# First stage of a four-layer graph network: where x is loaded, how the layernorms are ordered, and when the check of adj is written

## The chip, the core and the metric

The kernel runs on one core of one Trainium2 chip. The metric is the device time of a launch in microseconds, as the median of seven runs. The engines are named as the profile names them: PE (matrix products), DVE (vector), ACT (scalar activations), POOL (GpSimd) and SP (which here only issues DMAs).

## What is computed

Four layers work on x, 8 batches of 2048 nodes with 64 features, with a 0/1 matrix `adj` of 2048 x 2048. Each layer first normalises x. Cut to what this change touches:

```python
def _layernorm(x, axis=-1, eps=1e-5):
    m = jnp.mean(x, axis=axis, keepdims=True)
    v = jnp.var(x, axis=axis, keepdims=True)
    return (x - m) / jnp.sqrt(v + eps)

# layer 0
h = jnp.maximum(_layernorm(x, axis=-1), 0.0)
x = x + _L0_gnn_ref(h, L0_gnn_H, adj, 64, L0_gnn_W, ...)   # begins with h @ W
# layers 1, 2 and 3 follow in the same manner, each with adj
```

## The kernel before

The program has a first stage and a long rest. The first stage, `start` (L629), does three things: it normalises x for layer 0, multiplies the result by `W` (`features`, L669), and reads `adj` once to see whether it is sparse enough for a faster form of the layers (`check_adj`, L368). The check ends in one integer, `flag` (L423). Every engine loads the flag and branches on it (L3187, L3214), so that nothing of the rest begins before the flag is written and before that engine has done its own part of the first stage. The rest is not touched by the change.

**The layernorms.** x lies as 4 pairs of batches on 128 partitions and is cut into 4 chunks of 512 nodes. For each chunk `ch`, `load_x` (L262) loads 1 MB into the tile `x_ch` (two buffers), and `norm_parts` (L284) runs: for each of 4 pairs PE subtracts the mean by a product with `center`, ACT squares the result into `sq` (L291), and DVE or ACT in turn take its positive part `xr` (L294, L296); PE sums the squares (`to_rows`), ACT takes the root `std` (L299), DVE its reciprocal (L300). There the generator yields. Its second part spreads the reciprocal over the partitions by PE (`from_rows`) and multiplies on DVE (`write`, L641). Before, `norm` runs both parts without a stop, and `xr`, `sq` and `std` have one buffer each.

**The features.** For a chunk, PE multiplies by `ww` in two layouts, and ACT copies both out (L676 into `h_t`, L682 into `h_n`).

**The check of adj.** A loop over 16 row tiles of 1 MB. SP loads tile t into one of four halves of two buffers `rows` (L390). ACT squares it into `squares`, of which there are four (L391). DVE compares the square with the row (L392), which proves that the entries are 0 or 1. POOL clears the diagonal (L395) and issues the DMA that stores the tile as `links` in device memory (L399). PE counts blocks (`seen`). So the load of tile t + 4 waits for the compare of tile t, and the squares of tile t + 4 wait for the store of tile t. After the loop come small sums, two counting products, and `flag`.

**The order.** Each engine runs its instructions in a fixed order. A scheduler makes that order when the program is built: it takes the instructions in the order in which they are written as their rank, and lets a later one go first where it estimates that the engine would stand idle. In the kernel before, the loop over chunks was written first (with `features` of chunk ch - 1 after the layernorm of chunk ch), then the check, then `features` of the last chunk. SP's order before was: two loads of x, a load `own` of the diagonal (8 KB in pieces of 4 bytes), 2 rows of adj, x of chunk 2, 4 rows, x of chunk 3, 6 rows, `hm` (0.5 MB of H), 4 rows.

Of the kernel before, what the change touches and what calls it, by code (L numbers as in the profile page):

```python
# [7 lines left out]
F = mybir.dt.float32  # L8
# [11 lines left out]
P = 128  # L20
# [3 lines left out]
NP = NB // 2  # L24
NT = N // P
R = P // NP
CW = 512
NC = N // CW
TC = CW // P
# [106 lines left out]
class Kernel:  # L136
# [39 lines left out]
    def mm(self, out, lhsT, rhs, start=True, stop=True):  # L176
        self.nc.tensor.matmul(out, lhsT, rhs, start=start, stop=stop)  # L177
# [102 lines left out]
    def norm(self, *args):  # L280
        for _ in self.norm_parts(*args):
            pass
# [346 lines left out]
    def start(self, pool, slots):  # L629

        nc, tc, a = self.nc, self.tc, self.a
        self.deg = pool.tile([P, 2, NT], F, name="deg")
        self.edges = pool.tile([P, NT, FAR], BF, name="edges")
        self.self_weight = pool.tile([P, NT], F, name="self_weight")
        flag = pool.tile([1, 1], I32, name="flag")
        with tc.tile_pool(reuse_waits="tile", name="k00", bufs=1) as k:
            ww = self.block_diag(k, a["W"], "ww")
            hn = Halves(slots, "hn", ("q0", "q1"), False)

            def write(q, ch, xr, scale):  # L640
                nc.vector.tensor_mul(hn(q)[:, ch * CW : (ch + 1) * CW], xr, scale)  # L641

            with (
                tc.tile_pool(reuse_waits="tile", name="links_ps", bufs=1, space=PSUM) as lps,
                tc.tile_pool(reuse_waits="tile", name="ln", bufs=2) as w,
                tc.tile_pool(reuse_waits="tile", name="ln_ps", bufs=6, space=PSUM) as ps,
            ):
                seen = lps.tile([P, NT, FAR], F, name="seen")
                self.h = (
                    hn, Halves(slots, "h_t", ("q2", "q3"), False),  # L650
                    Halves(slots, "h_n", ("q4", "q5"), True),
                )

                def bank():
                    return ps.tile([P, CW], F, name="bank")

                for ch in range(NC):
                    x = self.load_x(w, 0, ch)
                    xr = w.tile([P, NP, CW], F, name="xr", bufs=1)
                    sq = w.tile([P, NP, CW], F, name="sq", bufs=1)  # L660
                    std = w.tile([P, CW], F, name="std", bufs=1)
                    self.norm(ch, x, xr, sq, std, bank, write)
                    if ch > 0:
                        self.features(ww, ch - 1, bank)
                self.check_adj(k, slots, seen, lps, flag)
                self.features(ww, NC - 1, bank)
        return flag

    def features(self, ww, ch, bank):  # L669
# [2612 lines left out]
```

## Time and profile before

| | |
|---|---|
| median of 7 runs | 1923.02 us |
| lowest and highest of the 7 | 1910.75 and 1927.65 us |
| the profiled execution: its time | 1915.7 us |
| its span, first to last instruction | 1913.9 us |
| PE, DVE, ACT, POOL busy over the span | 1685.5, 1380.1, 817.9, 1082.6 us |
| `flag` written in the trace | at 96.5 us |
| first stage's last PE product and last ACT copy | at 99.6 and 100.2 us |

Times inside the trace are microseconds from the start of the span. A row of the timeline view gives the start, the duration, the engine, the line, the operation, what it writes and reads, how many were merged (`x4`), and in brackets how long the engine stood idle before it and what ended that. The window view gives the busy time of each engine in a stretch, then the granted PE clock as a share of full speed, the share of the 16 DMA engines that was busy, and GB/s.

### The profile page before, as it was taken

What the parts mean: (1) busy time and instruction counts of PE and PEld (TensorE: products, weight loads), DVE (VectorE), ACT (ScalarE), POOL (GpSimd) and SP (SyncE); (2) the same over time, 40 slices, a digit from 0 to 9 for tenths busy, and PEclk for the clock granted to TensorE, in tenths of its full rate; (3) what the DMA queues carried; (4) which work ended last, traced back from release to release, by engine and by line L of the source; (5) the groups of instructions that cost most, each with busy time, mean ns of one, the idle gap of its engine ahead of it and who ended that gap; (6) DMA issues with size and microseconds to landing.
All of it is one profiled execution on the core that took longest, in us unless ns stands there. A gap on an engine that the chain in (4) does not pass through costs nothing.

```text
span 1913.9 us, 22584 instructions
## 1 busy us (share of the span) xinstructions
PE 1685.5 (88%) x7139; PEld 962.4 (50%) x7139; DVE 1380.1 (72%) x2281; ACT 817.9 (43%) x1650; POOL 1082.6 (57%) x1039
## 2 busy tenths in 40 slices
PE   6888899998997788899999999879999899599794
PEld 2446766664334454344343434258677576355442
DVE  6887778884667877778888877556566676478683
ACT  5732544554666654222111010067676754286200
POOL 1101366776862645887687766547373641587743
PEclk8998999998998889899999999999999999799896
DMA  8741223334545775234132242168788774766745
GB/s 335 293 124 46 67 94 99 112 123 163 178 125 153 213 223 159 86 86 132 39 110 88 72 116 77 51 215 272 240 253 263 227 246 146 247 183 184 209 142 190
DMA packets 127371, 305.25 MB, mean 159 GB/s; under 512 B 29680, under 2 KB 33536, under 8 KB 122112
## 3 DMA queue, kind: packets, MB, share of 16 engines
q0 software_dynamic: 45328, 149.60, 27.0%
q1 hardware_dynamic: 79600, 149.82, 23.4%
q10 hardware_dynamic: 2304, 4.20, 0.6%
q8 instruction: 60, 0.98, 0.2%
q14 instruction: 79, 0.65, 0.1%
HBM read 240.41 MB, written 63.14 MB: 159 GB/s over the span
## 4 chain that ended last, share of the span: by engine, by line
PE 33%; DMA 6%; issue 6%; POOL 6%; DVE 4%; ACT 1%; SPq 0%; POOLq 0%; DVEq 0%; ACTq 0%
PE pk L177 17%; PE acc L177 10%; POOL ring L2975 3%; DMA raw<-sent,index 2%; DMA ring<-f_rows,near 2%; PE bank L177 1%; POOL raw L2645 1%; PE pn L177 1%; POOL half L1872 1%; PE pw L177 1%; PE pz L1955 1%; PE side L177 1%; DMA ring<-f_rows,order 1%; PE p L177 1%; POOL q L3154 1%
## 5 line engine op out<-in xcount | busy, mean ns | idle before, releaser
L2645 POOL DMA_INDIRECT raw<-sent,index x300 | 315.9, 1053 | 286.6 <-DVE part_lo L2663 142.7
L2662 ACT CAST part_hi<-raw 128x512 fp32r<-128x512 f32 x352 | 210.8, 619 | 300.4 <-PE acc L177 203.0
L2663 DVE TENSOR_TENSOR part_lo<-raw,part_hi 128x512 fp32r<-128x512 f32 x352 | 264.9, 772 | 93.3 <-ACT part_hi L2662 86.3
L177 PE MATMUL pk<-q,w 128*128 128x512 f32 (+1 forms) x768 | 305.6, 615 | 4.2 <-DVE q L1753 2.7
L1872 POOL TENSOR_TENSOR half<-half,y 128x512 f32<-128x512 f32 x210 | 263.5, 1285 | 63.5 <-DVE y L1867 62.8
L177 PE MATMUL acc<-q,ident 128*128 128x512 f32 x416 | 204.2, 619 | 19.8 <-DVE q L3058 14.7
L177 PEld LDWEIGHTS pk<-q,w 128*128 128x128 f32 (+1 forms) x768 | 115.9, 191 | 155.0 <-issue 109.5
L177 PE MATMUL acc<-part_hi,weights 128*128 128x512 f32 x365 | 172.8, 474 | 21.8 <-ACT part_hi L2662 21.0
L177 PE MATMUL acc<-part_lo,weights 128*128 128x512 f32 x365 | 164.1, 451 | 24.6 <-DVE part_lo L2663 24.2
L2975 POOL DMA_INDIRECT ring<-f_rows,near x121 | 147.9, 1222 | 60.9 <-issue 28.6
L1867 DVE SCALAR_TENSOR_TENSOR y<-pk,bias,q 128x512 f32<-128x512 f32 x210 | 148.1, 743 | 43.8 <-POOL half L1872 23.5
L177 PEld LDWEIGHTS acc<-q,ident 128*128 128x128 f32 x416 | 78.6, 197 | 95.4 <-issue 63.5
L2354 POOL TENSOR_TENSOR q<-q,beta 128x512 f32<-128x512 f32 x57 | 76.0, 1335 | 71.4 <-DVE beta L2330 32.6
L177 PEld LDWEIGHTS acc<-part_lo,weights 128*128 128x128 f32 x365 | 71.5, 196 | 81.3 <-DVE part_lo L2663 68.0
L177 PEld LDWEIGHTS acc<-part_hi,weights 128*128 128x128 f32 x365 | 71.2, 195 | 74.3 <-ACT part_hi L2662 39.9
L177 PE MATMUL pp<-adj,x_ind_hi 128*128 128x512 f32 x256 | 90.2, 468 | 0.5 <-DVE q L882 0.3
L3040 DVE TENSOR_TENSOR q<-ring,e 128x1024 f32<-128x1024 f32 x58 | 70.1, 1221 | 10.6 <-PE acc L177 10.5
L2631 ACT CAST hub_weights<-dense 128x384 fp32r<-128x384 uint8 x80 | 40.4, 511 | 84.3 <-PE acc L177 84.0
L300 DVE RECIPROCAL std<-std 128x512 f32<-128x512 f32 (+1 forms) x17 | 53.8, 3162 | 30.4 <-ACT std L299 30.4
L2354 POOL TENSOR_TENSOR q<-q,coef 128x512 f32<-128x512 f32 x57 | 63.0, 1106 | 21.0 <-DVE q L2377 17.6
L2562 POOL DMA_INDIRECT listed_raw<-in_adjT_dram,cell x60 | 63.8, 1063 | 16.5 <-issue 15.9
L177 PE MATMUL pp<-adj,x_ind_lo 128*128 128x512 f32 x256 | 72.7, 403 | 0.0
(503 smaller groups left out, 3425.1 us busy)
## 6 DMA issues: line engine op xcount, KB each, us to landing
rows<-in_adj_dram SPq DMA_DIRECT2D x16, 1024.0 KB, 9.0
adj_t<-in_adjT_dram SPq DMA_DIRECT2D x64, 256.0 KB, 3.0
own<-sent SPq DMA_DIRECT2D x52, 256.0 KB, 4.2
raw<-sent SPq DMA_DIRECT2D x52, 256.0 KB, 3.6
sent<-u SPq DMA_DIRECT2D x48, 256.0 KB, 3.3
q<-x SPq DMA_DIRECT2D x9, 1024.0 KB, 4.9
links<-squares POOLq DMA_DIRECT2D x16, 512.0 KB, 8.6
sent<-q SPq DMA_DIRECT2D x32, 256.0 KB, 3.5
```

The costliest lines, as they stand in the source:

```text
L177: self.nc.tensor.matmul(out, lhsT, rhs, start=start, stop=stop)
L300: nc.vector.reciprocal(std, std)
L1867: nc.vector.scalar_tensor_tensor(y, pks[b, half], bias[:, b : b + 1], emb[:, b], op0=OP.add, op1=OP.mult,)
L1872: nc.gpsimd.tensor_add(acc, acc, y)
L2354: self.nc.gpsimd.tensor_tensor(x, x, by.unsqueeze(2).to_broadcast([P, NB, D]), op=OP.mult)
L2562: self.kern.behind(nc.gpsimd.indirect_dma_start(raw[:, i], None, rows, bass.IndirectOffsetOnAxis(ap=self.cell[:, c + i : c + i + 1], axis= ...
L2631: self.nc.scalar.copy(to, self.lists.dense[:, :, i * P : (i + 1) * P])
L2645: self.nc.gpsimd.indirect_dma_start(raw, None, self.rows[:], bass.IndirectOffsetOnAxis(ap=self.lists.index[:, c : c + 1], axis=0),)
L2662: nc.scalar.copy(hi, raw)
L2663: nc.vector.tensor_sub(lo, raw, hi.bitcast(F))
L2975: self.nc.gpsimd.indirect_dma_start(to, None, self.kern.f_rows[:], bass.IndirectOffsetOnAxis(ap=index, axis=0))
L3040: nc.vector.tensor_tensor(y.rearrange("n i (b f) -> n i b f", b=NB), block[:, i : i + 2, : NB * D].rearrange("n i (b f) -> n i b f", b=NB) ...
```

## The change

All four loads of x are written ahead of everything else, and go into the memory that `h_n` will fill later, so that the tile `x_ch` is gone. The first part of the layernorm of chunk ch + 1 is written before the second part of chunk ch; `xr` and `std` have two buffers for this. `features` of chunk 0 and 1 are written inside the loop, and those of chunks 2 and 3 after the check.

```diff
+                h_n = self.h[2].tiles
+                xs = [h_n[c // 2][:, TC * (c % 2) : TC * (c % 2 + 1)] for c in (1, 0, 2, 3)]
                 for ch in range(NC):
-                    x = self.load_x(w, 0, ch)
-                    xr = w.tile([P, NP, CW], F, name="xr", bufs=1)
+                    nc.sync.dma_start(xs[ch], self.xs[0][ch])
+
+                def norm(ch):
+                    xr = w.tile([P, NP, CW], F, name="xr")
                     sq = w.tile([P, NP, CW], F, name="sq", bufs=1)
-                    std = w.tile([P, CW], F, name="std", bufs=1)
-                    self.norm(ch, x, xr, sq, std, bank, write)
-                    if ch > 0:
+                    std = w.tile([P, CW], F, name="std")
+                    return self.norm_parts(ch, xs[ch], xr, sq, std, bank, write)
+
+                norms = [norm(0)]
+                next(norms[0])
+                for ch in range(NC):
+                    if ch + 1 < NC:
+                        norms.append(norm(ch + 1))
+                        next(norms[-1])
+                    for _ in norms[ch]:
+                        pass
+                    if 0 < ch < NC - 1:
                         self.features(ww, ch - 1, bank)
                 self.check_adj(k, slots, seen, lps, flag)
-                self.features(ww, NC - 1, bank)
+                for ch in range(NC - 2, NC):
+                    self.features(ww, ch, bank)
```

What the scheduler makes of it: on every engine the instructions behind the branch stand in the same order as before; all differences lie in the first stage. SP's order is now: four loads of x, `own`, 4 rows, `hm`, 12 rows. DVE's order (multiplies means the four of L641 of a chunk, r4 the compare L392 of row tile 4): xr 0, reciprocal 0, xr 1, reciprocal 1, multiplies 0, r0, xr 2, multiplies 1, reciprocal 2, r1, `hm` to 0/1, r2, half of xr 3, r3, other half of xr 3, reciprocal 3, multiplies 2, r4, sum of `hm`, r5, multiplies 3, r6, r7, r8 to r15 with three small ones between, then the small sums. Before it was: xr 0, r0, reciprocal 0, r1, multiplies 0, r2, half of xr 1, r3, other half, reciprocal 1, r4, multiplies 1, r5 to r7, xr 2, reciprocal 2, r8, multiplies 2, r9 to r11, xr 3, reciprocal 3, r12, multiplies 3, r13 to r15, the small sums. PE's products for `features` now all end before the small counting products; before, those of chunk 3 stood behind them.

## The prediction, made before the changed kernel ran

> **What bounds the kernel now.** On every engine the instructions behind the branch on `flag` stand in the same order before and after, so the question is when the first stage ends. I read the window view over that stage first.
>
> ```profile
> 20.00:40.00 20.00, 12.63 (x72) 4.83 (x72) 19.05 (x17) 14.21 (x19) 3.55 (x8) 0.67 0.97 369
> 40.00:60.00 20.00, 16.94 (x120) 9.17 (x116) 14.58 (x16) 14.97 (x22) 3.32 (x8) 0.92 1.01 419
> 60.00:80.00 20.00, 16.88 (x121) 9.03 (x121) 17.78 (x19) 16.30 (x25) 3.71 (x8) 0.91 0.96 327
> 80.00:100.00 20.00, 19.36 (x139) 12.71 (x140) 17.10 (x41) 12.73 (x20) 4.84 (x11) 0.91 0.30 122
> ```
>
> The DMA engines are full (0.96 to 1.01) up to 80 us and nearly empty after it, and DVE is busy for 14.6 to 19.1 of every 20 us. So there are two bounds with little between them: first the transfers, then DVE with what is left over. PE's clock is the next column: 0.67 from 20 to 40.
>
> Next the waits of the DMA queue and of ACT up to 100 us (total, times, longest).
>
> ```profile
> SPq L390 <- DVE equal L392: 46.5, 11, 8.9
> SPq L264 <- PE bank L177: 7.4, 2, 4.7
> ACT squares L391 <- DMA rows<-in_adj_dram: 8.6, 3, 5.8
> ```
>
> Eleven loads of adj wait for a compare on DVE: how early DVE gets to the compares decides how early the transfers run. Then the timeline, at the first norm and at the end.
>
> ```profile
> 4.91 6.53 SPq L390 DMA_DIRECT2D rows<-in_adj_dram  x2
> 15.96 1.91 ACT L391 ACTIVATE squares<-rows 128x2048 bf16<-128x2048 f32 x1 [1.99 <-DMA rows<-in_adj_dram]
> 17.86 0.58 ACT L291 ACTIVATE sq<-bank 128x512 f32<-128x512 f32 x1
> 17.99 2.29 DVE L392 SCALAR_TENSOR_TENSOR equal<-rows,squares 128x2048 bf16<-128x2048 f32 x1 [3.30 <-ACT squares L391]
> 20.96 3.35 DVE L300 RECIPROCAL std<-std 128x512 f32<-128x512 f32 x1 [0.67 <-ACT std L299]
> 26.48 2.48 DVE L641 TENSOR_TENSOR q<-xr,bank 128x512 f32<-128x512 f32 x4
> 61.99 11.18 SPq L390 DMA_DIRECT2D rows<-in_adj_dram  x4
> ...
> 89.56 2.42 DVE L392 SCALAR_TENSOR_TENSOR equal<-rows,squares 128x2048 bf16<-128x2048 f32 x1
> 96.50 0.14 DVE L423 TENSOR_SCALAR flag<-one 1x1 int32<-1x1 f32 x1
> 96.76 2.84 PE L177 MATMUL bank<-ww,q 128*128 128x128 f32 x24
> 99.64 0.59 ACT L682 COPY q<-bank 128x512 f32<-128x512 f32 x1 [0.31 <-PE bank L177]
> 100.17 0.37 DVE L518 COPY raw<-bank 128x208 f32<-128x208 f32 x1 [0.89 <-PE bank L177]
> ```
>
> ACT's fourth square of norm 0 (17.86) stood behind the square of adj's row 0, which waited for its transfer. The last row was issued near 73 and landed at 81.6, but DVE compared it only at 89.56, since norm 3 and three compares stood before it: the end is DVE's. And PE and ACT still finish features up to 100.2, past the flag at 96.64.
>
> **What the change removes, adds and moves.** I walk DVE's new order with these durations: compare 2.29 + 0.08 = 2.37; reciprocal 3.35; four multiplies 2.48; two positive parts 2 x 0.69 = 1.38.
>
> *Norm 0 and 1.* No row of adj stands in ACT's way now. The fourth product by `center` is out at 14.2, as before. Square and positive part (0.6 each) end at 15.4, the table load of 1.28 at 16.7, the root (0.69) at 17.4, the reciprocal at 20.9; it was 24.3. ACT's six operations for norm 1 (3.5) end at 20.9, its root at 22.3; DVE does xr 1 meanwhile and reciprocal 1 to 25.8 (it was 38.2). Multiplies 0 end at 28.2. So norms run 3 and 12 us earlier.
>
> *Rows 0 to 3.* Two more transfers of x are now ahead of row 0: 1 MB at the 400 GB/s of these windows is 2.6 to 2.75 us each, so row 0 lands at 21.4, not 15.9. That costs nothing by itself, for DVE comes to compare 0 only at 28.2 and ends it at 30.6, not at 20.3. That is the price: row 4 is issued 10 us later.
>
> *Rows 4 to 10.* From 30.6: xr 2 1.38, multiplies 1 2.48, reciprocal 2 3.35, compare 1 to 40.2; the test of `hm` 0.69, compares 2 and 3 with xr 3 to 47.0; reciprocal 3 to 50.3, multiplies 2 to 52.8, compare 4 to 55.2, the sum of `hm` 1.21, compare 5 to 58.8, multiplies 3 and compare 6 to 63.6. All of this is DVE back to back. In such a chain DVE also waits for ACT and PE: in the two windows from 20 to 60 it idled 0.95 and 5.42. From both sides 0 to 6.4; I take 1.5, near the fuller window, as DVE has more ready work now. Compare 6 ends at 65.1, and row 10 is issued then; in the trace row 10 was issued at 48.7. In between the DMA engines drain: rows 5, 6, 7 are issued at 40.2, 43.2 and 46.3, one MB each, and each MB is gone in 2.5 us.
>
> *Rows 10 to 15.* From here DVE has nothing but compares (2.37 each) and the transfers are late: a tile is 1.05 MB of row and 0.52 MB of links, at 419 GB/s 3.75 us. Row 10 takes 5.7 from issue to landing (as row 12 before, 61.99 to 67.7) and lands at 70.8; five more tiles at 3.75 put row 15 at 89.6. Square 2.0 and compare 2.5 end at 94.1. From the end of the last compare to the flag it was 91.99 to 96.64, 4.65: the flag at 98.8, 2.2 later. The rate is bounded by the 403 to 442 of single 2-us windows, 3.9 to 3.56 a tile: +0.8 to -1.0.
>
> A page states a lower ceiling. The Trainium skill, "DMA: Bandwidth & Descriptors", section "Bandwidth", gives about 358 GB/s as a core's share of device memory and 435 as the port limit; at 358 a tile would be an estimated 4.4 us and the flag 3.2 later still. The row's 419 over 20 us contradicts the share here and agrees with the port limit.
>
> *Features moved.* Those of chunks 2 and 3 are written after the check, but the scheduler puts them between rows, and they end before the last compares. PE and ACT are free at the flag, where before PE held up L518 for 0.89. Bounds 0 (the next DVE wait is for a load that SP issues after the flag anyway) and 3.5 (100.2 less 96.64); I take 0.5.
>
> *At no cost.* x in `h_n`'s memory: the copies L682 of chunk 0 overwrite x of chunk 1, which PE read before 20; if that cover went, the 4.0 us in which those copies already wait for PE would grow. SP's order: 4 rows and `hm` pass behind x and `own`; all land before DVE wants them. POOL's order is the same. The slot of the old `x_ch` wait (7.4 us on SP) goes, but rows wait behind DVE instead.
>
> *Sum.* +2.2 - 0.5 = +1.7 us. The profiled execution took 1915.7 for a span of 1913.9, so 1917.4; the seven runs have their median at 1923.02, so 1924.7. A measurement of this kernel can tell about 0.5%, 9.6 us, from no change.
>
> **The rivals.**
>
> *DVE stays fed, faster.* If the transfers never ran dry, DVE's own work would set the end: 16 x 2.37 + 4 x 7.21 + 3.2 for `hm` and small sums = 69.9, from 11.3 on, with 4.9 idle before reciprocal 0: 86.1, plus 4.65 is 90.8, 5.9 early; with the 0.5, 1916.6. For it: the norms are 12 us ahead, and the gaps before `std` are filled. Against it: no compare in 31 to 38, so one load every 3 to 10 us while four buffers are all there are.
>
> *PE at half clock, slower.* The place is 26 to 62, where DVE's multiplies 2 and 3 wait for PE behind `center` 2 and 3 and features 0 and 1. Eight rows of 128x512 take 0.43 each at full and 0.85 at half clock: +3.4 for each `center`, and the same and as much again for the 128x128 part of each feature group, 21 in all at most. It decides the sign from 7.9 us on, which brings 1.7 to 9.6. Take 12: 1936.7. For it: 0.50 from 20 to 28 and 36 to 42 in the trace. Against it: those came after PE had stood, and the new order gives PE unbroken work from 8.6.
>
> On that the Trainium skill, "TensorE: Matmul & The Clock Gate", section "HAM oscillation", asks for no PE idle gap over some 3.4 us. By it the rival falls if PE is fed, and the sum stays as it is; without it the 21 stands as the bound.
>
> *Far faster.* The DVE floor and the whole 3.5 of the features together give 9.4: 1913.6; more needs something outside the stage. *Nothing moves.* The scheduler had filled the gaps already: 1923.
>
> **How the numbers follow.** Forecast 0.56, DVE fed 0.18, half clock 0.12, far faster 0.07, nothing 0.07. Forecast, DVE fed and nothing lie within 0.5%: 0.81, less some for the scatter (the seven runs span 0.9%): faster 0.08, same 0.78, slower 0.14. The range: forecast's own ends are -1.5, -1.0 and -3.0 for waits, rate and features, and +4.9, +0.8 and +0.5 for the same: 1919.2 to 1930.9; to reach 8 in 10 I take in the DVE floor at 1916.6 and some of the half clock: 1916 to 1934.
>
> **What would show it.** Right: reciprocal 1 done near 26 but compare 0 only near 31; DMA share well under 0.9 somewhere in 30 to 65; near 1.0 from 67 to 89; rows 11 to 15 3.7 us apart; the last square starting as its row lands; flag at 97 to 101; no PE or ACT features after it. Wrong: the DMA share at 1.0 throughout with DVE the last to finish and the flag at 91 (the DVE floor); clock 0.5 over most of 26 to 62 and multiplies 3 ending past 70 (half clock); a stage behind the branch whose length differs by more than 5 us.

## The result, and the profile after

The changed kernel takes 1929.43 us (median of 30 runs, 1919.9 to 1937.06) where the kernel before takes 1918.95 (72 runs on the same chip, 1908.06 to 1930.46): 1.0053 of before, 95% interval 1.0042 to 1.0065, so 10 us slower. The forecast was 1924.7, 1.7 over the kernel before; the direction and most of the steps held, the size did not. The profiled execution has a span of 1919.5 us, 5.6 more than before, and the flag is written at 105.5 where it was at 96.6, so 8.9 later. Each profile is of a single execution: the one after took 7.9 less than its median, the one before 3.3 less.

First the window view of the changed kernel over the same four stretches.

```profile
20.00:40.00 20.00, 18.34 (x102) 7.24 (x101) 18.02 (x18) 16.42 (x24) 1.03 (x2) 1.00 0.79 276
40.00:60.00 20.00, 14.00 (x69) 6.61 (x68) 19.51 (x19) 13.76 (x21) 3.95 (x9) 0.88 0.79 272
60.00:80.00 20.00, 18.91 (x175) 13.59 (x173) 12.70 (x17) 14.20 (x22) 3.90 (x9) 0.95 0.74 274
80.00:100.00 20.00, 8.24 (x105) 6.97 (x102) 12.06 (x11) 13.53 (x18) 4.15 (x10) 0.65 0.90 374
```

The next to last column is the share of the DMA engines. Before it was 0.97, 1.01, 0.96 and then 0.30; now it is 0.79, 0.79, 0.74 and then 0.90. The same bytes go later. The same view in steps of 2 us shows where nothing moved, and what a full stretch looks like:

```profile
38.00:40.00 2.00, 2.00 (x15) 1.57 (x14) 2.00 (x2) 1.73 (x3) 0.00 (x0) 1.00 0.02 6
40.00:42.00 2.00, 2.00 (x21) 2.00 (x20) 2.00 (x3) 2.00 (x4) 0.00 (x0) 1.00 0.00 0
68.00:70.00 2.00, 1.97 (x5) 0.57 (x3) 2.00 (x2) 1.93 (x6) 0.00 (x0) 1.00 0.00 0
78.00:80.00 2.00, 1.81 (x19) 0.91 (x17) 0.35 (x3) 2.00 (x3) 0.83 (x2) 1.00 1.03 428
```

The timeline of DVE shows why (compare 0, 1, 4, 5, 6 and 15 are the rows of L392):

```profile
18.33 3.35 DVE L300 RECIPROCAL std<-std 128x512 f32<-128x512 f32 x1 [2.65 <-ACT std L299]
26.30 2.42 DVE L641 TENSOR_TENSOR q<-xr,bank 128x512 f32<-128x512 f32 x4
28.63 2.29 DVE L392 SCALAR_TENSOR_TENSOR equal<-rows,squares 128x2048 bf16<-128x2048 f32 x1
39.65 2.23 DVE L392 SCALAR_TENSOR_TENSOR equal<-rows,squares 128x2048 bf16<-128x2048 f32 x1
53.88 2.29 DVE L392 SCALAR_TENSOR_TENSOR equal<-rows,squares 128x2048 bf16<-128x2048 f32 x1
57.22 2.28 DVE L392 SCALAR_TENSOR_TENSOR equal<-rows,squares 128x2048 bf16<-128x2048 f32 x1
65.66 2.48 DVE L641 TENSOR_TENSOR q<-xr,bank 128x512 f32<-128x512 f32 x4 [6.15 <-PE bank L177]
68.06 2.29 DVE L392 SCALAR_TENSOR_TENSOR equal<-rows,squares 128x2048 bf16<-128x2048 f32 x1
99.14 2.29 DVE L392 SCALAR_TENSOR_TENSOR equal<-rows,squares 128x2048 bf16<-128x2048 f32 x1 [0.61 <-ACT squares L391]
105.38 0.14 DVE L423 TENSOR_SCALAR flag<-one 1x1 int32<-1x1 f32 x1
108.04 0.31 DVE L518 COPY raw<-bank 128x208 f32<-128x208 f32 x1
```

From 28.6 to 57 DVE goes through the order that the prediction walked, each step within 2 us of it. Then comes what the prediction had not: DVE stands 6.15 us ahead of multiplies 3. In the rows of ACT and PE that wait can be followed back.

```profile
55.44 1.91 ACT L391 ACTIVATE squares<-rows 128x2048 bf16<-128x2048 f32 x1 [4.21 <-DMA links<-squares]
57.34 1.54 ACT L690 COPY q<-bank 128x512 f32<-128x512 f32 x3
57.96 2.07 PE L177 MATMUL bank<-q,ww 128*128 128x512 f32 x2 [4.61 <-ACT q L690]
59.83 4.75 PE L177 MATMUL bank<-ww,q 128*128 128x128 f32 x32
64.50 1.14 PE L177 MATMUL bank<-std,from_rows 32*128 32x512 f32 x8
```

Read from the bottom: `from_rows` of chunk 3, which multiplies 3 need, stand behind `features` 1 on PE; these waited 4.61 for banks that ACT had to copy out; the copies (L690, in the other kernel L676) stood on ACT behind the square of row tile 6; and this square waited 4.21 for the store of tile 2, whose buffer of `squares` it takes. That store was issued at 45.87, since POOL clears the diagonal in place (L395) and so only after compare 2 (42.40). So a late compare holds back two rings, not one: the row load of tile t + 4, and by way of the store the square of tile t + 4. The waits of SP up to 100 us (total, times, longest), and those of the other engines up to 110:

```profile
SPq L390 <- DVE equal L392: 46.4, 9, 10.5
SPq L390 <- DVE least L442: 10.7, 1, 10.7
```

```profile
ACT squares L391 <- DMA links<-squares: 11.3, 6, 4.2
DVE equal L392 <- ACT squares L391: 9.6, 6, 3.1
DVE q L641 <- PE bank L177: 7.9, 3, 6.1
```

The first line seems to say that loads wait for compares as long as before (46.5). They do not: the one wait of 10.7 put down to L442 is that of row 10, which was issued at 70.38, as compare 6 ended; L442 is only the instruction that DVE ran next. And ACT's squares waited 8.6 for rows before; now they wait 11.3 for stores.

### The profile page after: what moved, and what is told of

Its sections match the earlier page's. It is cut to its first block, busy times and chain, and to the rows that moved or that the text cites. A ratio compares the mean times of both kernels' runs of the same rounds, so it can differ in the third digit from the quotient of the medians.

```text
span 1919.5 us, 22572 instructions
## 1 busy us (share of the span) xinstructions
PE 1691.5 (88%) x7139; PEld 968.4 (50%) x7139; DVE 1379.7 (72%) x2281; ACT 818.0 (43%) x1650; POOL 1077.3 (56%) x1039
## 4 chain that ended last, share of the span: by engine, by line
PE 39%; issue 5%; DMA 5%; POOL 4%; DVE 3%; ACT 1%; DVEq 0%; POOLq 0%; SPq 0%; ACTq 0%
PE pk L177 17%; PE acc L177 13%; DMA raw<-sent,index 2%; POOL ring L2989 2%; PE bank L177 1%; PE pn L177 1%; PE first L177 1%; PE pw L177 1%; POOL raw L2659 1%; PE pz L1969 1%; PE side L177 1%; DMA ring<-f_rows,near 1%; POOL half L1886 1%; PE p L177 1%; PE plain L177 1%
```

## The experiments

Behind the branch on the flag, every version below has the same order of instructions as the kernel before. The experiments ran on four chips: on two of them the kernel before took about 1919 us, on two about 1997, so times are compared only as ratios to before on the same chip. `flag` is the end of the row that writes it. The chips differ behind the flag: from there to the end the traces have 1814 to 1824 us on the faster chips and 1892 to 1903 on the slower. Each flag is from one execution, though, and PE's granted clock differed between them: from 30 to 45 us it was 1.0 throughout in the changed kernel, with six rows, with row tiles 0, 4, 4, 4, and in the two versions with norms in two parts alone; in the others and in the kernel before it was 0.5 for some 7 us or more of that stretch.

| version | flag, us | ratio to before, 95% interval |
|---|---|---|
| before | 96.64 | 1 |
| **the changed kernel** | 105.52 | 1.0053 (1.0042 to 1.0065) |
| x loaded first, alone | 98.01 | 1.0019 (0.9993 to 1.0046) |
| norms in two parts, alone | 104.87 | 1.0046 (1.0016 to 1.0076) |
| changed, `features` 2 back in the loop | 105.33 | 1.0043 (1.0015 to 1.0070) |
| changed, 6 squares | 103.71 | 1.0046 (1.0013 to 1.0080) |
| changed, 6 rows | 105.39 | 1.0063 (1.0042 to 1.0083) |
| changed, 6 rows and 5 squares | 105.34 | 1.0043 (1.0020 to 1.0066) |
| changed, row tiles written 0, 4, 4, 4 | 95.19 | 0.9994 (0.9969 to 1.0018) |
| the same, `own` written behind row 8 | 98.05 | 0.9989 (0.9966 to 1.0012) |
| changed, row tiles written 2, 2, 4, 4 | 97.34 | 0.9996 (0.9977 to 1.0015) |
| the same, 6 rows and 5 squares | 100.24 | 1.0007 (0.9981 to 1.0034) |
| row tiles 0, 4, 4, 4, 6 rows and 5 squares | 94.08 | 0.9978 (0.9955 to 1.0001) |
| norms in two parts alone, row tiles 0, 4, 4, 4 | 97.43 | 1.0011 (0.9989 to 1.0034) |

### Which part costs

**x loaded first, alone** (norms in one piece, `features` as before):

```diff
 # before
+                h_n = self.h[2].tiles
+                xs = [h_n[c // 2][:, TC * (c % 2) : TC * (c % 2 + 1)] for c in (1, 0, 2, 3)]
+                for ch in range(NC):
+                    nc.sync.dma_start(xs[ch], self.xs[0][ch])
+                for ch in range(NC):
-                    x = self.load_x(w, 0, ch)
...
-                    self.norm(ch, x, xr, sq, std, bank, write)
+                    self.norm(ch, xs[ch], xr, sq, std, bank, write)
```

> The kernel before with one part of the change alone: all four loads of x first, into h_n's memory; layernorms whole and features as before. Theory A (late compares: the split layernorms keep DVE from the compares, the loads of adj wait for it, and the transfers run dry): the rows land later by the 5.5 us of two transfers of x, but compares 0 and 1 run near 24 and 28, so the flag is at 97 to 100 and the time within 0.2% of before. Rival B (the loads themselves: 2 MB more ahead of the first row shift everything by 5.5 us and more): flag at 102 or later, time 0.3 to 0.5% above before. Rival C (a store of links holds up ACT's queue, and the features and PE behind it): no statement beyond B or A; a wait of multiplies 3 for PE of over 3 us would speak for it.

Flag at 98.0, ratio 1.0019, its interval on both sides of 1. That is theory A's range. The four loads in front are not what costs: DVE has compare 0 at 24.71 and compare 1 at 28.71.

**Norms in two parts, alone** (`xr` and `std` with two buffers, loads and `features` as before; the edit is shortened):

```diff
 # before
-                    self.norm(ch, x, xr, sq, std, bank, write)
+                norms = [norm(0)]; next(norms[0])
+                    # in the loop: first part of ch + 1, then second part of ch
```

> The kernel before with another part alone: the first part of the layernorm of chunk ch + 1 is written before the second part of chunk ch; x is loaded chunk by chunk through two buffers as before, and features as before. Theory A: as slow as the whole change or slower, since rows 0 and 1 come early but compares 1 and 2 stand behind layernorms 1 and 2: flag at 103 to 107, time 0.3 to 0.6% above before; the DMA share falls below 0.5 somewhere between 30 and 45. Rival B: flag at 95 to 98, time as before. Rival C: between the two, with multiplies 3 waiting for PE.

Flag at 104.87, ratio 1.0046: nearly the whole effect. The windows show the same picture as in the changed kernel, with DMA shares far under those of before, and from 40 to 44 the share falls to 0.16 and 0.00:

```profile
40.00:60.00 20.00, 19.40 (x106) 11.14 (x105) 19.05 (x20) 15.30 (x25) 3.65 (x8) 1.00 0.71 251
60.00:80.00 20.00, 18.01 (x183) 13.00 (x179) 14.29 (x17) 14.19 (x20) 3.32 (x8) 1.00 0.69 249
```

Here compare 0 is as early as before (17.94), but compare 1 comes at 31.75 and compare 2 at 40.75: the steps of the norms that the split makes ready stand ahead of them.

**`features` of chunk 2 back inside the loop:**

```diff
 # the changed kernel
-                    if 0 < ch < NC - 1:
+                    if ch > 0:
                         self.features(ww, ch - 1, bank)
-                for ch in range(NC - 2, NC):
-                    self.features(ww, ch, bank)
+                self.features(ww, NC - 1, bank)
```

> The changed kernel with features of chunk 2 written inside the loop again, as before; only chunk 3's stand after the check. Theory A and rival B: the flag within 2 us of the changed kernel's 105.5 and the time within 0.15% of it, since neither the compares 0 to 7 nor the loads move. Rival C: up to 3 us either way, as ACT's copies stand differently against the squares.

Flag at 105.33, ratio 1.0043: 0.2 us at the flag. The place of `features` is worth nothing that can be told here.

### Is it the number of buffers?

**Six buffers of squares** (in memory of their own), so that the square of tile t waits for the store of t - 6:

```diff
 # the changed kernel
-        squares = slots.tile([P, 4, N], BF, name="squares", tag="q8")
+        squares = pool.tile([P, 6, N], BF, name="squares")
...
-            row, sq = rows[t // 2 % 2][:, t % 2], squares[:, t % 4]
+            row, sq = rows[t // 2 % 2][:, t % 2], squares[:, t % 6]
```

> The changed kernel with six buffers of squares in place of four, so that the square of row t waits for the store of links of row t - 6 and not t - 4. Rival C (in the changed kernel's trace the square of row 6 waits until 55.4 for a store, four copies of features stand behind it, and multiplies 3 wait 6.2 us for PE): that wait falls to under 1 us, multiplies 3 start near 60, and the flag comes at 99 to 102. Theory A alone: the last rows are spaced by the transfers at 3.7 us whatever the squares do; flag at 103 to 106. Rival B: 105.

The 6.15 us wait ahead of multiplies 3 is gone (62.51 instead of 65.66), so the chain read above is right. The flag, though, moves by 1.8 only, into theory A's range and not rival C's: the last rows are still loaded late, one every 3.7 us. DVE's waits between compares 0 and 6 are 5.1 (0.43, 1.92, 1.85 and 0.90) instead of 7.9. The 1.85 and 0.90 are new, and this trace differs in PE's clock too; the window from 34 to 40, here and in the changed kernel:

```profile
34.00:40.00 6.00, 6.00 (x10) 2.19 (x7) 4.72 (x4) 1.50 (x3) 0.00 (x0) 0.50 0.40 142
34.00:40.00 6.00, 6.00 (x26) 3.31 (x26) 4.82 (x4) 3.62 (x6) 0.00 (x0) 1.00 0.48 173
```

The first eight products of `features` 0 took 6.46 here and 3.70 there, and ACT's `sq` of norm 3, for which DVE waited 1.85, stand behind their copies. Whether the second ring would be worth more than 1.8 at full clock is not shown; the version with `features` 2 back had the half clock too (33.5 to 40.3), and its flag was at 105.33.

**Six buffers of rows**; squares stay four, in memory of their own, since the rows take theirs:

```diff
 # the changed kernel
-        rows = [... for i in range(2)]
+        rows = [... for i in range(3)]
-        squares = slots.tile([P, 4, N], BF, name="squares", tag="q8")
+        squares = pool.tile([P, 4, N], BF, name="squares")
...
-            row, sq = rows[t // 2 % 2][:, t % 2], squares[:, t % 4]
+            row, sq = rows[t // 2 % 3][:, t % 2], squares[:, t % 4]
```

> The kernel after with six buffers for rows instead of four (squares stay four, in memory of their own). The order of DVE is nearly the same, so the compares are as late as they were, but the load of tile t + 6, not t + 4, waits for compare t. Theory A: tiles 4 and 5 are loaded right behind tile 3, so the empty stretch at 38 to 42 fills up, the 5 to 6 us that DVE stood before multiplies 3 shrink or go, and the flag comes at 100 to 103. Rival C (squares and links): squares are as few as before and their stores now meet more loads, flag at 104 to 107.

Flag at 105.39, ratio 1.0063. Theory A had said 100 to 103 and missed, rival C's 104 to 107 held: rows 4 and 5 were indeed loaded early, but their squares started at 40.29, after 3.35 us of waiting for a store, and at 52.71, after 5.05 in which POOL's clearing is named; both stand behind compares 0 and 1 all the same. This is what brought out the second ring.

**Six rows and five squares**, both rings looser:

```diff
 # the changed kernel
-        rows = [... for i in range(2)]
+        rows = [... for i in range(3)]
-        squares = slots.tile([P, 4, N], BF, name="squares", tag="q8")
+        squares = pool.tile([P, 5, N], BF, name="squares")
...
-            row, sq = rows[t // 2 % 2][:, t % 2], squares[:, t % 4]
+            row, sq = rows[t // 2 % 3][:, t % 2], squares[:, t % 5]
```

> The kernel after with six buffers for rows and five for squares. In the traces POOL's clearing of the diagonal waits for the compare, since both use the same squares; so a late compare holds back two rings: the load of tile t + 4 and, through the store of links, the square of tile t + 4. Six rows alone left the flag at 105.25 and six squares alone at 103.6. Theory A, now for both rings: with both loosened and the compares written as late as they were, the transfers of rows go on through 38 to 42 and DVE stands less than 3 us ahead of multiplies 3; flag at 97 to 102, time 0.997 to 1.003 of before. Rival C' (the stores, squeezed between the loads of rows, hold ACT up however many squares there are): flag at 103 to 106, time 1.003 to 1.007. Rival D (the split order itself makes DVE wait for PE and ACT): flag at 103 to 106 with DVE idle more than 5 us between 40 and 70.

Flag at 105.34, ratio 1.0043: theory A missed again; the range of rivals C' and D, which is the same, held. The timelines of POOL, ACT and DVE:

```profile
44.70 0.57 POOL L399 DMA_DIRECT2D links<-squares  x1 [0.31 <-POOL squares L395]
52.70 1.91 ACT L391 ACTIVATE squares<-rows 128x2048 bf16<-128x2048 f32 x1 [5.14 <-issue]
57.91 3.35 DVE L300 RECIPROCAL std<-std 128x512 f32<-128x512 f32 x1 [5.26 <-ACT std L299]
```

Compare 1 is at 39.67 as it was, so the store of tile 1 goes out at 44.70; tile 6 takes its buffer, and its square starts at 52.70. On ACT the last `sq` and `std` of norm 3 stand behind that square, and DVE stands 5.26 us for `std`. That the square waited for that store is inferred from the order and from the 6.2 to 9.0 us that such stores took in the changed kernel; this trace names no releaser for it. So a larger ring does not help while one engine comes to the compares late: ACT has squares and norms in one queue, and a square that waits holds up the norm.

### Is it the place of the compares?

**Row tiles written in between**, 0, 4, 4 and 4 ahead of the second parts of the four norms, the last 4 behind the loop; rings, loads and `features` as in the changed kernel:

```diff
 # the changed kernel; check_adj yields after each row tile
+                check = self.check_adj(k, slots, seen, lps, flag)
...
+                    for _ in range((0, 4, 4, 4)[ch]):
+                        next(check)
                     for _ in norms[ch]:
                         pass
...
-                self.check_adj(k, slots, seen, lps, flag)
+                for _ in check:
+                    pass
```

> The kernel after, with the 16 row tiles of the check written in between: four ahead of the second part of the layernorm of chunk 1, four ahead of that of chunk 2, four ahead of that of chunk 3, four behind the loop. DVE's order up to compare 0 stays; compare 1 then comes right behind the positive part 2, and the compares are spread between the multiplies. Theory A (compares written last come late, the loads wait for them, the DMA engines run dry, and the end is then set by 3.7 us per tile): compare 1 near 32.5 where it was 39.65, no empty 2 us window between 36 and 70, flag at 94 to 100 where it was 105.4, time 0.995 to 1.001 of before. Rival C (ACT's squares wait for the stores of links, and the features' copies stand behind them): the stores and the features are as many as they were, so DVE still stands for 5 us or more before multiplies 3 and the flag stays at 103 to 106, time 1.003 to 1.006. Rival D (DVE's work is simply as long as the stage): its sum is the same, flag at 103 to 106.

Flag at 95.19, ratio 0.9994: the 10 us are gone, with four rows and four squares. Rivals C and D, which kept the flag at 103 to 106, fall. The edit moves whole row tiles, the square on ACT and the store included, so it shows the place of these steps together, not that of the compare alone. Compare 0 is where it was in the changed kernel, and compare 1 comes right behind it; the largest wait of DVE from there to the flag is now 1.69:

```profile
28.91 2.28 DVE L392 SCALAR_TENSOR_TENSOR equal<-rows,squares 128x2048 bf16<-128x2048 f32 x1
32.32 2.28 DVE L392 SCALAR_TENSOR_TENSOR equal<-rows,squares 128x2048 bf16<-128x2048 f32 x1
65.28 0.69 DVE L642 TENSOR_TENSOR q<-xr,bank 128x512 f32<-128x512 f32 x1 [1.69 <-PE bank L177]
```

And the windows are full again until the rows end:

```profile
40.00:60.00 20.00, 16.85 (x100) 7.94 (x99) 19.20 (x20) 16.63 (x25) 4.43 (x11) 1.00 0.97 354
60.00:80.00 20.00, 18.98 (x172) 13.33 (x173) 15.79 (x18) 14.98 (x23) 4.35 (x11) 1.00 1.00 402
```

In one point theory A was wrong: it had said no empty 2 us between 36 and 70, which holds, but 30 to 32 has a share of 0.23, the hole that compare 0 at 28.9 leaves.

**The same with `own` written behind row 8:**

```diff
 # row tiles written 0, 4, 4, 4
-        nc.sync.dma_start(own, ...)          # ahead of the rows
+            if t == 8:
+                nc.sync.dma_start(own, ...)  # written behind row 8
```

> As the version with the row tiles written four by four, and the load of own (8 KB in 4-byte pieces, behind which SP stood 8.85 us at row 0) moved behind row 8 on SP. Theory A: the rows land some 5 us earlier, but DVE comes to compare 0 no earlier, so the flag moves by less than 1.5 us against the version without it: 93 to 100. Rival E (the block of SP behind own sets the start of the whole chain): flag 4 us or more earlier than the version without it. A third possibility: 2048 small pieces between full rows cost the transfers 2 to 4 us later on, flag later by as much.

The order that the scheduler made is not the one written: SP issued `own` at 10.11, behind row 3, and the long issue, 8.86 on row 0 where `own` stands just ahead of it, now fell on `hm` (15.13). Rival E, that SP's stand behind `own` sets the start of everything, is tested all the same: row 0 landed at 19.18 instead of 21.42, but compare 0 moved by 0.8 only, and the flag came at 98.05, 2.9 later (ratio 0.9989). So rival E falls, and theory A's bound of 1.5 was missed. The third possibility gave the right size, but not by its cause, small pieces among full rows: `own` had landed at 27.77, before row 4 was issued (30.42). What did it is not shown. DVE waits 4.20 for PE up to 70.44, and PE, at work without a gap from 46.6 to there, had a clock of 0.5 from 54.2 to 64.5, where the version above had 1.0 up to 86.5: six products of 128x512 took 4.94, as many elsewhere in the same trace 2.82. DVE's order differs a little too. In time the two versions cannot be told apart.

**Row tiles written 2, 2, 4, 4:**

```diff
-                    for _ in range((0, 4, 4, 4)[ch]):
+                    for _ in range((2, 2, 4, 4)[ch]):
```

> The kernel after with the row tiles written 2, 2, 4 and 4 ahead of the second parts of the four layernorms, the last four behind the loop. DVE then has compare 0 ahead of multiplies 0, and compare 1 right behind the first of them. Theory A: compare 0 near 26, compare 1 near 29, compare 2 near 34; flag at 94 to 100, time 0.995 to 1.001 of before. Rivals C and D: flag 103 to 106, time 1.003 to 1.006.

Flag at 97.34, ratio 0.9996: the same cure by another pattern.

**Norms in two parts alone, row tiles 0, 4, 4, 4** (x and `features` as before):

```diff
 # norms in two parts, alone
-                self.check_adj(k, slots, seen, lps, flag)   # behind the loop
+                # written 0, 4, 4 and 4 ahead of the second parts, 4 behind the loop
```

> The version with the split norms alone (loads of x and features as before; alone its flag came at 104.9 and its time was 1.0046 of before), with the row tiles of the check written 0, 4, 4 and 4 ahead of the second parts of the four layernorms, the last four behind the loop; rings as before. Theory A, as it stands after the runs on buffers (what costs is where the compares stand in the order of DVE, and the squares in that of ACT, among the steps of the norms, not the number of buffers): compare 1 stays near 32, but the compares from 4 on come some 3.5 us apart with a multiply or two in between, and the flag comes at 93 to 98, time 0.995 to 1.001 of before. Rival F (the split needs x loaded first, and without it each x waits behind rows on SP): flag at 100 to 105, time 1.001 to 1.005.

Flag at 97.43 against 104.87 without it: theory A's range for the flag, and rival F's 100 to 105 falls. The ratios, 1.0011 against 1.0046, lean the same way, but their intervals overlap, and 1.0011 lies at the border between the two theories. So the split costs through the place of the row tiles' steps, and x need not be loaded first for the cure.

### Is there more to gain?

**Row tiles 2, 2, 4, 4 with six rows and five squares** (the edits of both versions above):

> The kernel after with the row tiles written 2, 2, 4 and 4 ahead of the second parts of the layernorms (alone: flag 97.2, time 0.9996 of before) and with six rows and five squares. Theory A: with early compares and looser rings the transfers stay near full from 24 us to the last row; flag at 90 to 95, time 0.994 to 0.999 of before. Rival D (DVE's own work bounds it from here on): flag at 94 to 97, time 0.997 to 1.001.

Flag at 100.24, ratio 1.0007; both theories missed. The last compare was done at 90.8, but PE was late: DVE then waited 5.17 for PE's `seen`. On PE the last products of `features` stand ahead of these sums. They had waited 2.89, up to 85.40, for copies on ACT, which stood behind a square that itself waited 3.99 and started at 82.87; and PE's clock was 0.5 from 84.6 to 91.4.

**Row tiles 0, 4, 4, 4 with six rows and five squares:**

> The kernel after with the row tiles written 0, 4, 4 and 4 ahead of the second parts of the layernorms (alone: flag 95.2, time 0.9994 of before) and with six rows and five squares. Theory A: two more rows are loaded before compare 0 ends at 31, so the stretch at 28 to 34, in which the transfers ran dry, fills; flag at 90 to 94, time 0.994 to 0.999 of before. Rival D: flag at 94 to 97, time 0.997 to 1.001.

Flag at 94.08, ratio 0.9978 (0.9955 to 1.0001). The hole at 28 to 34 did fill: from 30 to 40 the share is 1.01. The flag lies at the border between theory A's range and rival D's. It is the fastest version here: faster than the changed kernel, since the intervals are apart, but against the kernel before no more than a lean.

## Why the prediction was right, and where its size was off

**The number, partly luck.** The measured 1929.43 is 4.7 above the forecast of 1924.7, but the change is 10.5 and not 1.7: the seven runs from which the forecast starts have a median 4.1 above that of the 72. The flag came 8.9 later and not 2.2. Of the prediction's own signs, reciprocal 1 near 26, compare 0 near 31 and the DMA share under 0.9 came; the flag at 97 to 101 and full transfers from 67 to 89 did not (from 66 to 70 the shares are 0.13 and 0.00, and they are full from 76 to 96).

**The bound, right.** Behind the branch the order is the same, and the time follows the flag. A straight line through the 13 versions of the table (ratio times 1919 us against flag) gives 1.18 us of time for each us of flag and no change at 97.2, with no version more than 3.1 us off it.

**Norms 0 and 1, right.** Reciprocal 0 ended at 21.7 (said: 20.9), reciprocal 1 at 26.4 (25.8), multiplies 0 at 28.7 (28.2).

**Rows 0 to 3, right.** Compare 0 ended at 30.9 (30.6) and row 4 was issued at 30.95, against 20.32 before: the 10 us of the forecast. Rows 5, 6 and 7 were issued at 41.95, 44.86 and 47.80 (40.2, 43.2, 46.3).

**The step that failed: 1.5 us for DVE's waits on ACT and PE up to compare 6.** They were 0.43 + 1.34 + 6.15 = 7.9, over even the upper bound of 6.4. The value was taken from windows of before in which every store of `links` went out with an early compare. The prediction followed the late compares to the row loads, and not to POOL's clearing of the diagonal, the store, the square on ACT and what is queued behind it, here the copies of `features` 1 and so PE's products for multiplies 3. Compare 6 ended at 70.4 instead of 65.1: 6.4 more of waits, 0.3 of a later start, less 1.5, since instructions behind one another overlap a little (multiplies 0 run to 28.72, compare 0 starts at 28.63).

**Rows 10 to 15, right in kind, 2.1 short.** Row 10 was issued at 70.38 and landed at 76.30, 5.9 later (5.7), and compares 11 to 14 are 3.7 apart, as said. But from the end of compare 6 to that of compare 15 it was 31.1, not 29.0: the squares there wait for stores too. Square 10 started at 77.67, 1.4 behind its row, and square 11 came 5.45 behind square 10. The sums behind compare 15 took 4.1 instead of 4.65. Together: 5.3 + 2.1 - 0.6 = 6.8 us, but for rounding the difference between 98.8 and 105.5 at the flag.

**The rate, right.** The ten 2-us windows from 76 to 96 have a mean of 424 GB/s. The Trainium skill, "DMA: Bandwidth & Descriptors", section "Bandwidth", says in its note on single-core numbers that 358 GB/s is the share when both cores of a pair stream, and shows 425 for a core alone; the windows agree with the latter. The 3.2 us that the prediction worked out for 358 did not come.

**`features` moved, 0.5, not to be told.** L518 no longer waits for PE and comes 2.5 behind the flag instead of 3.5. From flag to end the profiled executions have 1817.3 before and 1814.0 after, so 3.3 less, near the upper bound; but from version to version on the faster chips, with the same order behind the flag, that stretch varies from 1814.0 to 1823.6. Moving `features` 2 back made no difference.

**The rivals.** *DVE stays fed* named the argument against itself, no compare between 31 and 38, and it decided. *Half clock* had its price, but as an effect: between 26 and 62, PE's clock was 0.5 only from 55.1 to 61.9, from 1.7 us into the 4.61 that PE stood waiting for ACT. The 32 products of 128x128 at 59.83 took 4.75; the same 32 of chunk 0, at 38.62, took 3.73 at full clock, so about 1 us of the 6.15, and as much for the two products ahead of them. *Far faster* and *nothing moves* are out: the interval of the ratio is 1.0042 to 1.0065.

The Trainium skill, "TensorE: Matmul & The Clock Gate", section "HAM oscillation", asks for no idle gap of PE over some 3.4 us. The prediction took from it that the rival falls if PE is fed, and these traces do not bear that out. In the changed kernel the clock was 0.5 again from 85.8 to 109.7, with no gap of PE over 2.4 there or in the 20 us before. With six squares it fell at 33.9, where PE's longest gap since 8.6 was 1.66. The kernel before has the same: the clock fell at 36.3, in a gap of 1.89. The measurement decides: the half clock came with a gap of 4.61, but gaps that stay under 3.4 do not rule it out.

## What to carry to other kernels

When an operation frees a buffer, follow everything that waits for it, through every engine, until the next buffer: here a compare on DVE freed the row and, by way of POOL's in-place step and the store, the square on ACT. Starting the next stage's first half early fills gaps only as long as the work that releases loads keeps its turn; where a scheduler takes the order of writing as rank, write the releasing steps in between, and look at buffers after that. Waits read from a trace belong to its order; a sum for another order needs bounds from its own chains.

## What the hardware showed unexpectedly

A store of 0.5 MB on POOL's queue took 6.2 to 9.0 us from issue to landing between 42 and 57 us of the changed kernel, while 1 MB loads went on SP's queue; alone, at the end of the kernel before's rows (issued 83.00, landed 85.91), it took 2.9. That is no effect of the change: beside loads the stores of the kernel before took 6.5 to 11.0. There they went out early enough that only one square waited for one (1.6); now they go out late, and six wait (11.3). The Trainium skill, "DMA: Bandwidth & Descriptors", section "Queues, rings and completion order", says that a DMA engine takes turns between the queues with work, packet by packet. No run here shows the turns themselves; the rows show the time: beside the loads, the store that a later square waits for took 3 to 6 us more than alone.
